# Graph attention on gathered neighbours: weighing a tile as a head and a tail, lists two tiles ahead, products from the last slot

## The chip, the cores and the metric

The kernel runs on one core of one Trainium2 chip. The metric is the device time of one execution in microseconds; it was taken three times for the kernel before. All engines have queues of their own, which run in order: TensorE (PE, its weight loads PEld), VectorE (DVE), ScalarE (ACT), GpSimd (POOL) and SyncE (SP).

## The reference

There are N = 4096 nodes with D = 128 numbers each, and a 0/1 matrix `adj` of which about 0.8% is set, so a row has some 32 neighbours. Layer 0 is graph attention with 8 heads, layer 1 takes quantiles over the neighbours' new values:

```python
Wh = einsum('nd,hde->hne', nodes, W)
f1, f2 = einsum('hnd,hd->hn', Wh, a1), einsum('hnd,hd->hn', Wh, a2)
e = leaky_relu(f1[:, :, None] + f2[:, None, :], 0.2)
att = softmax(where(adj > 0, e, -9e15), axis=-1)
h = elu(einsum('hnm,hmd->hnd', att, Wh))
cat = transpose(h, (1, 0, 2)).reshape(N, 8 * 128)
x1 = layernorm(nodes + elu(cat @ W1 + b1)) * gamma + beta
# layer 1: of each row's neighbours those at every ceil(n/2)-th place are removed;
# of the rest, for each of 128 columns, the values at the quantiles .25, .5, .75
out = s @ Wl.T + bl + x1      # s: half their mean, half the node's own x1
```

## The kernel before

The neighbours of a row are found first (`neighbours`, with `eights` and `best`: VectorE's MAX8 on keys that TensorE makes in PSUM, lines 561 to 614), as a record `rec` of up to 64 neighbour numbers, their count, the row's number and its f1. Rows are then ranked by their count (`rank_by_count`) and scattered to DRAM in that order, so that a tile of 128 rows has rows of nearly equal counts and few empty slots. This is done in three blocks of 4, 9 and 19 tiles (`BLOCKS`), and each tile has a fixed capacity (`CAPS`), rounded up to slots of 32, 16, 8 and 4 (`layers`): from 24 to 64 slots, 1180 in all.

Layer 0 of a tile has these steps:

- `read_lists` (line 767) loads the tile's records `R` (and `narrow` for layers under 32) on SP's queue, and VectorE turns them into index columns `idx` and the factors `f1x` (lines 776 to 809).
- `fetch_rows` (818) has POOL issue one indirect DMA (`gather`, line 178) for each slot: 128 rows of 136 numbers (x, and f2 of 8 heads) into one of 16 places of a buffer `G`. There are 6 such buffers.
- `attend` (843) weighs them. VectorE makes `z` = f1 + f2 and the leaky relu (858, 864), ScalarE its exp (865); TensorE sums it (`den`, 871), VectorE inverts (881, 882), TensorE spreads the inverse (`rz`, 886), VectorE multiplies (895) and spreads z to `wide` (902), one for each layer of slots. TensorE then makes one product for each slot (`y`, 913), which is the weighted sum of x. From there on the tile has 8 heads x 128 columns: in two halves of four heads, ScalarE copies y (927), TensorE multiplies with W (`hT`, 934), ScalarE and VectorE make the elu (943, 945, 946), and TensorE multiplies with W1 into `o` (948). `finish_x1` (969) adds and normalizes; POOL scatters x1 to DRAM (`x_d`, line 187).

`attend` is a generator that yields between steps. `step` (340) fetches one tile, then runs `attend` of the tile before from its beginning to its end. Within it, after the first yield, the lists of the tile after the fetched one are made (`soon`), and after each yield some pieces of another generator are run: the search for the next block's neighbours in blocks 0 and 1, and the lists of layer 1 (`lists_of_layer_1`, line 1009) in the last tiles of block 2. The pieces of a step (`quota`) are shared evenly over `STEPS` = 18 yields. DVE, PE, ACT and POOL run their instructions in the order in which they are written here (`manual_schedule`), so the order of these yields is the order of each queue.

PSUM is shared out so: `small` (den, then o) twice, `rz` once, `y` two banks, `hT` one, the keys two.

After layer 0 comes the sort: POOL gathers x1 rows of the neighbours (`vals`), and VectorE runs selection networks on them (`quantile_out`, line 1113). 

Of the kernel before, what the change touches and what calls it, by code (L numbers as in the profile page):

```python
# [9 lines left out]
F32 = mybir.dt.float32  # L10
BF16 = mybir.dt.bfloat16
I32 = mybir.dt.int32
AF = mybir.ActivationFunctionType
# [20 lines left out]
ROUNDS = L // 8  # L34
GROUP = 5
STEPS = 18
KEEP_MIN = 6.0
# [164 lines left out]
def kernel(  # L202
# [116 lines left out]

    weigh, store = [], []  # L320

# [17 lines left out]

    def step(fetch=None, soon=None, pieces=None, quota=0, first=False, among=()):  # L340
        if first:
            keep_x1(fetch)
        if fetch:
            weigh.append(fetch_rows(tc, attp, fetch, xt_d, list(among)))
        if not first:
            keep_x1(fetch)
        if len(weigh) > 1 or (weigh and not fetch):
            done = 0
            each = quota / STEPS
            for k, x1_t in enumerate(attend(tc, attp, pp, weigh.pop(0), consts)):  # L350
                if soon:
                    ready.append(prepare(*soon))
                    soon = None
                while done < min(quota, (k + 1) * each):
                    next(pieces, None)
                    done += 1
            store.append(x1_t)
            quota -= done
        if soon:
            ready.append(prepare(*soon))  # L360
        for _ in range(quota):
            next(pieces, None)
# [8 lines left out]
    with tc.manual_schedule(engines=ORDERED):  # L371
# [3 lines left out]
        for b, n in enumerate(BLOCKS):  # L375
# [12 lines left out]
            for i in range(n):  # L388
                among = []
                if last and 1 < i < n - 6:  # L390
                    among = [
                        (all_d, rec[:, t, 0:REC1], ranks[:, t : t + 1])
                        for t in range((i - 2) * NT // (n - 8), (i - 1) * NT // (n - 8))
                    ]
# [372 lines left out]
def read_lists(tc, ap, rec_d, i, cap, t, bad, narrow):  # L767
# [3 lines left out]

    R = ap.tile([P, REC], F32, name="R", bufs=4)
    rows = rec_d[ts(i, P), :]
# [4 lines left out]
    )  # L778
    mine = ap.tile([P, 1], I32, name="mine", bufs=7)
# [64 lines left out]
def attend(tc, ap, pp, fetched, consts):  # L844
# [7 lines left out]

    z = ap.tile([P, L, H], F32, name="z")
    layer = []
# [12 lines left out]

    den = pp.tile([P, 32 * H], F32, name="small", bufs=2)
    for i, (w, k, runs, f1v) in enumerate(parts):
# [9 lines left out]
    yield  # L879
    rden = ap.tile([4, 32 * H], F32, name="rden")  # L880
    nc.vector.tensor_scalar(rden, den[0:4, :], TINY, None, ALU.max)
# [17 lines left out]
    for i, (w, k, runs, f1v) in enumerate(parts):  # L899
# [9 lines left out]
        c = k * H  # L909
        for G, col, g0, m in runs:  # L910
            for g in range(g0, g0 + m):

                nc.tensor.matmul(  # L913
                    yf[:, ts(g, c)],
                    lhsT=G[:, col + g - g0, 0:D],
                    rhs=pf[:, ts(g, c)],
                    start=(i == 0 and g % (w // 2) == 0),
                    stop=(i == len(parts) - 1),
                    skip_group_check=True,
                )  # L920
                if g % 8 == 7:
                    yield

    o = pp.tile([P, 32 * H], F32, name="small", bufs=2)[:, 0:D]
    for h0 in range(0, H, 4):
        yT, hv, e = (ap.tile([P, 4, P], F32, name="half", bufs=4) for _ in range(3))
        nc.scalar.copy(  # L927
            yT.rearrange("p h (u g) -> p g u h", u=4),
            yf.rearrange("p (g u h) -> p g u h", u=4, h=H)[:, :, :, h0 : h0 + 4],
        )  # L930
        yield
        hT = pp.tile([P, 512], F32, name="hT")
        for h in range(4):
            nc.tensor.matmul(  # L934
                hT[:, ts(h, P)],
                lhsT=consts["W_sb"][:, h0 + h, :],
                rhs=yT[:, h, :],
                start=True,
                stop=True,
            )  # L940
        yield
        ef, hf = (v.rearrange("p h q -> p (h q)") for v in (e, hv))
        nc.scalar.activation(ef, hT, AF.Exp)  # L943
        yield
        nc.vector.tensor_scalar(ef, ef, 1.0, -1.0, ALU.min, ALU.add)  # L945
        nc.vector.tensor_tensor(hf, hT, ef, ALU.max)  # L946
        for h in range(4):
            nc.tensor.matmul(  # L948
                o,
                lhsT=hv[:, h, :],  # L950
                rhs=consts["W1_sb"][:, h0 + h, :],
                start=(h0 + h == 0),
                stop=(h0 + h == H - 1),
            )
        yield
    x1_t = ap.tile([P, D], F32, name="x1_t", bufs=4)
    yield from finish_x1(tc, ap, o, R[:, R_X : R_X + D], x1_t, consts)
# [429 lines left out]
```

## Time and profile before

| what | us |
|---|---|
| median of 3 runs (lowest, highest) | 3876.51 (3872.57, 3877.78) |
| the profiled execution: time, span | 4780.24, 4778.5 |
| z of tile 0 (end of setup) | 227 |
| z of tile 4 (block 1 begins) | 612 |
| z of tile 13 (block 2 begins) | 1444 |
| layer 0 ends, the sort begins | 2850 |
| busy: PE, DVE, ACT, POOL | 1355.3, 2676.4, 413.3, 2763.5 |

The profiled execution is one other execution, with the profiler on, and took 904 us more than the median. Times of single instructions and waits come from it. "A <- B" after an instruction's idle time says what ended the idle time: B, or "issue" where the profile shows no wait that ended just then, or "remote" where it can't tell the source. Ends of matmul records are modelled. A group of instructions is named by its line, engine, operation and tiles, with their shape.

### The profile page before, as it was taken

Reading aid. Unit: us, or ns where it says so; the run is one execution under the profiler, and the core shown is the slowest. Engines: PE = TensorE matmul, PEld = TensorE weight load, DVE = VectorE, ACT = ScalarE, POOL = GpSimd, SP = SyncE. Lnnn points to the kernel's source line nnn. Section 1 sums busy time; section 2 is a strip of 40 time slices with the busy share of each in tenths; the row PEclk is TensorE's granted clock in tenths of the full one; section 3 lists DMA queues with packets and bytes.
Section 4 is the critical chain, followed back from the end, with each engine's and each line's share of the span. In section 5 each row is a group of like instructions: output and inputs, shape, how many; then the busy total and the mean of one; then the engine's idle time right before and its main releaser. Section 6 shows DMA issues by size and latency. Waiting matters only on the chain. (4 is left out here: it accounts for less than half of the span.)

```text
span 4778.5 us, 22122 instructions
## 1 busy us (share of the span) xinstructions
PE 1355.3 (28%) x5429; PEld 1026.7 (21%) x5433; DVE 2676.4 (56%) x6455; ACT 413.3 (9%) x667; POOL 2763.5 (58%) x2388
## 2 busy tenths in 40 slices
PE   5373445556233443343424250000000000000010
PEld 2042333333232342232423240000000000000010
DVE  7463354554313111111134235687779999999868
ACT  2110111211000101100000010000000000000000
POOL 1534434334544454544444518888878888888883
PEclk9995555555555555555555555555555555555555
DMA  5321323321111111111111101111111111111110
GB/s 182 113 72 40 115 77 95 99 79 47 45 42 35 37 41 35 39 36 39 43 36 31 40 8 43 40 40 37 39 41 41 37 30 33 41 40 37 36 40 20
DMA packets 110282, 241.26 MB, mean 50 GB/s; under 512 B 46976, under 2 KB 63360, under 8 KB 101952
## 3 DMA queue, kind: packets, MB, share of 16 engines
q0 software_dynamic: 76160, 160.24, 12.5%
q10 hardware_dynamic: 9360, 67.18, 4.1%
q1 hardware_dynamic: 24624, 12.34, 1.1%
q8 instruction: 45, 0.74, 0.1%
q14 instruction: 93, 0.76, 0.1%
HBM read 228.44 MB, written 11.15 MB: 50 GB/s over the span
## 5 line engine op out<-in xcount | busy, mean ns | idle before, releaser
L178 POOL DMA_INDIRECT G<-xt_d,idx x1180 | 1130.7, 958 | 1285.2 <-issue 692.4
L178 POOL DMA_INDIRECT vals<-x_d,idx x1024 | 1423.4, 1390 | 314.5 <-issue 303.2
L1113 DVE TENSOR_TENSOR work<-work 128x256 f32<-128x256 f32 (+7 forms) x1168 | 922.0, 824 | 0.7
L913 PE MATMUL y<-wide,G 128*128 128x32 f32 (+3 forms) x2360 | 540.2, 410 | 234.2 <-DVE wide L902 137.9
L1113 DVE TENSOR_TENSOR work<-work,work 128x512 f32<-128x512 f32 (+4 forms) x820 | 584.7, 739 | 1.3
L1133 PE MATMUL st_ps<-dg,goal 128*128 128x128 f32 x286 | 71.1, 425 | 1794.4 <-DVE goal L1113 1430.9
L913 PEld LDWEIGHTS y<-wide,G 128*128 128x128 f32 x2360 | 516.8, 328 | 267.4 <-DVE wide L902 150.1
L945 DVE TENSOR_SCALAR half<-half 128x512 f32<-128x512 f32 x64 | 27.6, 432 | 915.3 <-ACT half L943 822.3
L1133 PEld LDWEIGHTS st_ps<-dg,goal 128*128 128x128 f32 x286 | 63.0, 321 | 1800.4 <-issue 1799.5
L563 DVE MAX8 first<-key 128x8 f32<-128x128 f32 x1024 | 228.0, 283 | 300.9 <-remote 132.6
L1113 DVE TENSOR_TENSOR work<-vals 128x768 f32<-128x768 f32 (+11 forms) x64 | 128.8, 2028 | 269.6 <-DMA vals<-x_d,idx 266.0
L948 PE MATMUL small<-W_sb,half 128*128 128x128 f32 x512 | 120.8, 410 | 484.7 <-DVE half L946 315.7
L596 PE MATMUL key<-sgn,markb 128*128 128x512 bf16 x255 | 151.0, 593 | 254.1 <-DVE first L563 105.0
L948 PEld LDWEIGHTS small<-W_sb,half 128*128 128x128 f32 x512 | 102.9, 298 | 503.9 <-DVE half L946 331.0
L934 PE MATMUL hT<-half,W_sb 128*128 128x128 f32 x512 | 116.1, 400 | 236.3 <-ACT half L927 143.7
L557 ACT ACTIVATE sgn<-adj_t 128x2048 bf16<-128x2048 int32 x64 | 122.1, 1907 | 555.0 <-PE key L596 387.1
L927 ACT COPY half<-y 128x512 f32<-128x512 f32 x64 | 65.5, 1023 | 1073.7 <-remote 536.5
L934 PEld LDWEIGHTS hT<-half,W_sb 128*128 128x128 f32 x512 | 103.9, 301 | 252.0 <-ACT half L927 153.6
L886 PE MATMUL rz<-rden,ownT 4*128 4x32 f32 (+3 forms) x436 | 112.3, 434 | 152.8 <-DVE rden L882 113.8
L599 PE MATMUL key<-parts,oneb 64*128 64x512 bf16 x256 | 149.1, 583 | 9.0 <-POOL parts L196 6.3
L1132 ACT ACTIVATE dg<-ident,wt 128x128 f32<-128x128 f32 x143 | 47.5, 393 | 1092.5 <-PE st_ps L1133 1008.4
L886 PEld LDWEIGHTS rz<-rden,ownT 4*128 4x128 f32 x436 | 98.4, 322 | 170.9 <-DVE rden L882 124.6
(178 smaller groups left out, 1773.0 us busy)
## 6 DMA issues: line engine op xcount, KB each, us to landing
adj_t<-in_adj_dram ACTq DMA_DIRECT2D x64, 1024.0 KB
G<-xt_d,idx POOLq DMA_INDIRECT x1180
vals<-x_d,idx POOLq DMA_INDIRECT x1024
R<-rec_d SPq DMA_DIRECT2D x128, 26.2 KB
xt_d<-rec SPq DMA_DIRECT2D x4, 544.0 KB
rec<-in_x_dram SPq DMA_DIRECT2D x4, 512.0 KB
W_sb<-in_L_gnn_W_dram SPq DMA_DIRECT2D x2, 512.0 KB
a_b<-in_L_gnn_a_dram SPq DMA_DIRECT2D x2, 512.0 KB
```

The lines of the kernel that those rows point to most:

```text
L178: nc.gpsimd.indirect_dma_start(out=dst, out_offset=None, in_=rows, in_offset=bass.IndirectOffsetOnAxis(ap=idx, axis=0),)
L557: nc.scalar.activation(sgn, adj_t, AF.Sign, accum_out=cnt[:, i : i + 1])
L563: nc.vector.max(first[:, ts(c0 // CW + c, 8)], key[:, ts(c, CW)])
L596: nc.tensor.matmul(key, lhsT=markb, rhs=sgn[:, ts(b, 512)], start=True, stop=False)
L599: nc.tensor.matmul(key, lhsT=oneb[0:64, :], rhs=parts[:, ts(r, 512)], start=False, stop=True)
L886: nc.tensor.matmul(rz[:, layer[i] * H : (layer[i] + w) * H], lhsT=ownT[w][:, r, :], rhs=rden.rearrange("p (g r h) -> p r g h", r=k // 4, h ...
L913: nc.tensor.matmul(yf[:, ts(g, c)], lhsT=G[:, col + g - g0, 0:D], rhs=pf[:, ts(g, c)], start=(i == 0 and g % (w // 2) == 0), stop=(i == le ...
L927: nc.scalar.copy(yT.rearrange("p h (u g) -> p g u h", u=4), yf.rearrange("p (g u h) -> p g u h", u=4, h=H)[:, :, :, h0 : h0 + 4],)
L934: nc.tensor.matmul(hT[:, ts(h, P)], lhsT=consts["W_sb"][:, h0 + h, :], rhs=yT[:, h, :], start=True, stop=True,)
L948: nc.tensor.matmul(o, lhsT=hv[:, h, :], rhs=consts["W1_sb"][:, h0 + h, :], start=(h0 + h == 0), stop=(h0 + h == H - 1),)
L1113: nc.vector.tensor_tensor(slots_of(dst, (j, c, s, m), size), slots_of(a, (i, c, s, m), size), slots_of(b, (i + d, c, s, m), size), op,)
L1133: nc.tensor.matmul(st_ps[:, u, :], lhsT=goal[:, (j * k + u) * D : (j * k + u + 1) * D], rhs=dg, start=(j == 0), stop=False,)
```

## The change

`attend` keeps its steps up to the products, then yields the word "summed"; what follows is the tail. In `step`, the tail of one tile and the head of the next are run in turns, one yield each, tail first, and the pieces after each turn. The tail works on all 8 heads at once: one copy of y of 128x1024, one exp, one elu, in two buffers `late`; hT has two banks of PSUM, and den and o share one PSUM tile `small`, made once. Lists are made two tiles ahead (`soon` names tile i + 2, and at the start of a block two tiles), for which `R`, `mine`, `idx` and `f1x` get more buffers. The products of a layer of slots run from the last slot to the first. `GROUP` (tiles whose records are completed at once) goes from 5 to 4, `STEPS` from 18 to 12. The lists of layer 1 start one tile later, and there is one more empty step at the end.

```diff
-GROUP = 5
-STEPS = 18
+GROUP = 4
+STEPS = 12
...
+    consts["small"] = pp.tile([P, 512], F32, name="small")
...
+            head = attend(tc, attp, pp, weigh.pop(0), consts)
+        active = [v for v in (tail.pop() if tail else None, head) if v]
+        k = 0
+        while active:
+            for v in list(active):
+                said = next(v)
+                if said == "summed":
+                    tail.append(v)
+                    active.remove(v)
+                elif said:
+                    store.append(said)
+                    active.remove(v)
+            ready.extend(prepare(*v) for v in soon)
+            soon = ()
+            k += 1
+            while done < min(quota, k * each):
+                next(pieces, None)
+                done += 1
...
-                soon = (b, i + 1, t0) if i + 1 < n else None
+                soon = [(b, j, t0) for j in ((1, 2) if i == 0 else (i + 2,)) if j < n]
...
-                if last and i == n - 6:
+                if last and i == n - 5:
...
-                    left = -(-LIST_PIECES // 5)
+                    left = -(-LIST_PIECES // 4)
...
-        for _ in range(4):
+        for _ in range(5):
             step()
...
-    R = ap.tile([P, REC], F32, name="R", bufs=4)
+    R = ap.tile([P, REC], F32, name="R", bufs=5)
...
-        idx = ap.tile([P, 32], I32, name="idx", bufs=6)
+        idx = ap.tile([P, 32], I32, name="idx", bufs=8)
...
-            f1x = ap.tile([P, H * 32], F32, name="f1x", bufs=7)
+            f1x = ap.tile([P, H * 32], F32, name="f1x", bufs=9)
...
-    den = pp.tile([P, 32 * H], F32, name="small", bufs=2)
+    small = consts["small"]
+    den = small[:, 0 : 32 * H]
...
-        for G, col, g0, m in runs:
-            for g in range(g0, g0 + m):
+        for G, col, g0, m in reversed(runs):
+
+            for g in reversed(range(g0, g0 + m)):
...
-                    start=(i == 0 and g % (w // 2) == 0),
+                    start=(i == 0 and g % (w // 2) == w // 2 - 1),
...
-                if g % 8 == 7:
+                if g % 8 == 0:
                     yield
...
+    yield "summed"
+
+    yT, hv = (ap.tile([P, H, P], F32, name="late", bufs=2) for _ in range(2))
+    nc.scalar.copy(
+        yT.rearrange("p h (u g) -> p g u h", u=4), yf.rearrange("p (g u h) -> p g u h", u=4, h=H)
+    )
+    yield
+    hT = pp.tile([P, 2, 512], F32, name="hT").rearrange("p a b -> p (a b)")
+    for h in range(H):
+        nc.tensor.matmul(
+            hT[:, ts(h, P)], lhsT=consts["W_sb"][:, h, :], rhs=yT[:, h, :], start=True, stop=True
+        )
+    yield
+    hf = hv.rearrange("p h q -> p (h q)")
+    nc.scalar.activation(hf, hT, AF.Exp)
+    yield
+    nc.vector.tensor_scalar(hf, hf, 1.0, -1.0, ALU.min, ALU.add)
+    nc.vector.tensor_tensor(hf, hT, hf, ALU.max)
+    o = small[:, 32 * H : 32 * H + D]
+    for h in range(H):
+        nc.tensor.matmul(
+            o, lhsT=hv[:, h, :], rhs=consts["W1_sb"][:, h, :], start=(h == 0), stop=(h == H - 1)
+        )
```

More of the change, by code (lines that the diff above doesn't have):

```diff
@@ L315 @@
     pp = tc.alloc_tile_pool(name="att_ps", bufs=1, space=PSUM)
-    weigh, store = [], []
+    weigh, store, tail = [], [], []
+    consts["small"] = pp.tile([P, 512], F32, name="small")
     narrow = {
@@ L338, in keep_x1, with step @@
             scatter(nc, x1_d, x1_t, r)
-    def step(fetch=None, soon=None, pieces=None, quota=0, first=False, among=()):
+    def step(fetch=None, soon=(), pieces=None, quota=0, first=False, among=()):
         if first:
@@ L346, in step @@
             keep_x1(fetch)
+        done = 0
+        each = quota / STEPS
+        head = None
         if len(weigh) > 1 or (weigh and not fetch):
[L348 to L360, printed above, removed]
+            head = attend(tc, attp, pp, weigh.pop(0), consts)
[16 more added lines that the diff above has]
+                done += 1
+        quota -= done
+        ready.extend(prepare(*v) for v in soon)
         for _ in range(quota):
@@ L389 @@
                 among = []
-                if last and 1 < i < n - 6:
+                if last and 2 < i < n - 5:
                     among = [
                         (all_d, rec[:, t, 0:REC1], ranks[:, t : t + 1])
-                        for t in range((i - 2) * NT // (n - 8), (i - 1) * NT // (n - 8))
+                        for t in range((i - 3) * NT // (n - 8), (i - 2) * NT // (n - 8))
                     ]
@@ L778, in read_lists @@
     )
-    mine = ap.tile([P, 1], I32, name="mine", bufs=7)
+    mine = ap.tile([P, 1], I32, name="mine", bufs=9)
     nc.vector.tensor_copy(mine, R.bitcast(I32)[:, R_OWN : R_OWN + 1])
@@ L850, in attend @@
     slots = sum(w for w, _, _, _ in parts)
-    z = ap.tile([P, L, H], F32, name="z")
+    z = ap.tile([P, L, H], F32, name="z", bufs=2)
     layer = []
@@ L879, in attend @@
     yield
-    rden = ap.tile([4, 32 * H], F32, name="rden")
+    rden = ap.tile([4, 32 * H], F32, name="rden", bufs=1)
     nc.vector.tensor_scalar(rden, den[0:4, :], TINY, None, ALU.max)
@@ L920, in attend @@
                 )
-                if g % 8 == 7:
+                if g % 8 == 0:
                     yield
[L924 to L929, printed above, removed]
-        )
[L931 to L955, printed above, removed]
@@ L956, in attend @@
-    x1_t = ap.tile([P, D], F32, name="x1_t", bufs=4)
+    yield "summed"
[8 more added lines that the diff above has]
+            hT[:, ts(h, P)], lhsT=consts["W_sb"][:, h, :], rhs=yT[:, h, :], start=True, stop=True
+        )
@@ L957, in attend @@
+    yield
[9 more added lines that the diff above has]
+        )
+    yield
+    x1_t = ap.tile([P, D], F32, name="x1_t", bufs=3)
     yield from finish_x1(tc, ap, o, R[:, R_X : R_X + D], x1_t, consts)
```

## The prediction

> **What bounds the kernel now.** I read the stretches first: each engine's busy time in setup, in the three blocks of tiles (the last block in two), and in the sort. Columns: stretch and length in us; busy us and instructions of PE, PEld, DVE, ACT, POOL; PE clock; DMA share; GB/s.
> ```profile
> 227.00:612.00 385.00, 197.20 (x717) 131.19 (x719) 182.75 (x686) 58.86 (x68) 161.31 (x168) 0.70 0.26 79
> 612.00:1444.00 832.00, 398.49 (x1464) 266.26 (x1465) 367.70 (x1356) 121.82 (x143) 346.23 (x360) 0.54 0.23 68
> 1444.00:2418.00 974.00, 365.15 (x1672) 327.83 (x1673) 185.68 (x450) 87.58 (x117) 495.96 (x513) 0.53 0.16 39
> 2418.00:2850.00 432.00, 179.06 (x810) 163.63 (x810) 166.61 (x645) 39.35 (x53) 154.95 (x163) 0.53 0.11 27
> ```
> No engine is full before 2850, so a chain of waits sets the pace there. The diff touches nothing after 2850 (sort, 1928 us). Block 0 is four tiles, block 1 nine (92 us each), the third stretch tiles 13 to 25 (75 us each), the fourth tiles 26 to 31 (72 us each).
>
> Second, the waits: who waited for whom, total us, times, longest.
> ```profile
> DVE half L945 <- ACT half L943: 822.3, 41, 77.5
> POOL G L178 <- issue: 692.4, 1124, 54.5
> POOL G L178 <- PE y L913: 540.2, 21, 56.6
> ```
> VectorE stands in the second half of a tile (L945), and behind it in its queue stand the next tile's z and the lists of the tile after. POOL stands for a G buffer that products must free (540 us), or for lists. Of the 692 us, about 1100 x 0.30 us = 330 is the fixed gap of each gather; the rest is waits for lists.
>
> Third, the timeline of tile 20, with gathers running, and of the last tile, with none.
> ```profile
> 1961.20 0.42 ACT L865 ACTIVATE z<-z 128x256 f32<-128x256 f32 x1 [1.27 <-DVE z L864]
> 1962.15 0.96 POOL L178 DMA_INDIRECT G<-xt_d,idx  x1 [17.96 <-issue]
> 1968.21 13.86 PE L913 MATMUL y<-wide,G 128*128 128x32 f32 x64 [1.84 <-DVE wide L902]
> 2006.17 1.01 ACT L927 COPY half<-y 128x512 f32<-128x512 f32 x1 [44.56 <-remote]
> 2018.83 0.60 ACT L943 ACTIVATE half<-hT 128x512 f32<-128x512 f32 x1 [11.65 <-remote]
> ...
> 2817.72 13.86 PE L913 MATMUL y<-wide,G 128*128 128x32 f32 x64 [1.84 <-DVE wide L902]
> 2831.62 1.02 ACT L927 COPY half<-y 128x512 f32<-128x512 f32 x1 [20.30 <-PE y L913]
> 2844.02 0.29 DVE L974 TENSOR_TENSOR v<-small,vecs 128x128 f32<-128x128 f32 x1 [1.25 <-PE small L948]
> ```
> Both records say 13.86 us for 64 product records. In the last tile the copy follows at once; in tile 20 it starts 24 us later, and tile 20's gathers for the next tiles fill that time. So TensorE finishes late while gathers run: 38 us for 13.9, a factor of 2.75.
>
> [...] That would make the lag a matter of profiling. The trace does not prove it, but the time speaks for it: the profiled execution took 4780.24 us, the median of three unprofiled runs is 3876.51, 904 us less. [...]
>
> **So two sums.** With TensorE at its unhindered pace, a 32-slot tile takes what the last one took: z at 2809.3, copy at 2831.6 (22), end at 2847.7 (16), 38 us. POOL needs 0.95+0.30 = 1.25 us an instruction: 513 x 1.25 = 641 us for tiles 13 to 25, 49 a tile, more than 38. There POOL is the pace, and 974 shrinks by 333. Block 1: POOL 360 x 1.25 / 9 = 50 a tile; VectorE 41. A tile costs between 50 and 38 + 33 (the searching, 294 us / 9, with nothing hidden), I take 56 plus 60 in all for the block's records: 832 shrinks by some 270. Block 0 likewise by 80, the fourth stretch by 80. Together 760 of the 904; the sort may give the rest. This fits, so I forecast on the unhindered sum, against 3876.51; the sum as profiled is given as a rival.
>
> **Part by part.**
> 1. *Tail beside the next head.* Nothing is removed from the tail: two copies of 1.02 become one of 2.04, two exps of 0.60 one of 1.19, L945 2 x 0.43, L946 2 x 0.69 become about 0.86 and 1.23, 8 + 8 weight products stay 32 records x 0.213 = 6.8 us. Estimated from z to the last product: 22 us alone, plus hT's 3.4 us ahead of den on TensorE, plus 0.86 + 1.23 on VectorE and o's 3.4 ahead of the products, less overlap: 28. On ScalarE the copy's 2.04 stands ahead of the head's exp; it is within the 3.4. The pace of the chain is 28 instead of 38. The scatter of x1 (1.0 us on POOL) is issued one step later, and nothing waits for it before the sort: 0.
>  Block 1: from 56 to 51, since POOL's 50 is next: 9 x 5 = 45. Block 0: 4 x 6 = 24 by the same share. Tiles 13 to 25: 0, POOL is hidden by nothing. Tiles 26 to 31: list pieces are 98 us of VectorE, some 16 a tile; 38 to 45 + part of 16 is above POOL's 34 (163 x 1.25 / 6), so 4 tiles x 7 = 28. The last tile: head 28 beside tail 30, then its own tail 16, but it starts 16 earlier: 9 less. Gain: 106.
> 2. *Lists two tiles ahead.* Takes away POOL's waits for lists (17.96 in the line above). With POOL as pace they are already gone: 0 beyond part 1. The DMAs are as many (R four issues, 1.7 us on SP; narrow four, 1.3 us) and stand on SP's queue with nothing else; R is kept for the tail and has a fifth buffer, so no load waits for it. VectorE's 2.2 us of transposes stay in front of rden. But the ring idx has 8 buffers and tiles 14 to 16 take 3 each, so list 16 waits for 16 gathers of tile 14, 16 x 1.25 = 20 us, VectorE behind it with rden. Once; between 0 and 20, I take 10.
> 3. *Products from last to first.* 0 in TensorE's time. G's first buffer comes free after 32 products instead of 16, 16 x 0.427 = 6.8 us later. Hidden as long as head + gather < two tiles: 28 + 50 < 100. The waits themselves: the records run at 0.213 with and without one, so 0.
> 4. *GROUP 4.* One more group in blocks 1 and 2, 24 small VectorE instructions of about 0.2 each: 2 x 4.8, hidden if POOL is the pace. Between 0 and 10, I take 5. *STEPS 12* only shares the pieces over fewer turns; what is left after the last turn runs beside the next copy: 0, at worst two pieces of 2 us a step, 13 x 4 = 52.
> 5. *PSUM:* hT takes two banks, den and o share one tile. den of the next head must wait until v (L974) has read o; that is a full head earlier: 0.
>
> Sum: 106 - 10 - 5 = 91 less; 3876.5 - 91 = 3785. I say 3783, as the ends are rounded.
>
> **Rivals.**
> A. *TensorE lags beside gathers without a profiler too.* For it: the trace shows it in every tile. Against: the sort cannot give 904 us by itself without VectorE's 1649 us of it shrinking by more than half. As profiled, a tile costs gather time plus the TensorE work that it could not do meanwhile: tiles 13 to 25: 24 us of work, 49 + 24 - 49/2.75 = 55 against 75, 13 x 20 = 260; block 1: 42 of work, 74 against 92, 160; elsewhere 100. 520 of 4780, 11%. Half true, 5 to 7%: 3876 - 250 = 3630.
> B. *The gathers set the pace everywhere.* Then parts 1 and 2 only shorten what was hidden; 3876 + 0 to 15, about 3880. For it: POOL's 50 a tile in block 1 is close to my 56. Against: 60 us of VectorE per tile in block 0 can't be hidden in 52.
> C. *Slower: G comes free too late.* The place is POOL's wait for y, in the 18 tiles with over 32 slots, which need three buffers or more of six. A gather starts when the first buffer of two tiles back is free, lasts 50, and the head needs it. With a head stretched by pieces, as in blocks 0 and 1, the pace is half of gather + 2 + head; it passes 56 when the head passes 60 us. The trace has 43 to 85 us from z to the copy in block 1 (though with TensorE lagging). Price 18 x 6.8 / 2 = 61 at least where two tiles share a delay, 122 where each pays it, with some of part 1's gain left: 3876 + 40 = about 3915.
>
> **How the numbers follow.** Forecast (3700 to 3860): 0.48. A (3560 to 3700): 0.25. B: 0.12, mostly within 0.2%. C: 0.15. About 0.2%, 8 us, is what a measurement of this kernel can tell from no change. Faster: 0.48 + 0.25 and a little of B, 0.74; same 0.09; slower 0.17. Range 3610 to 3895: it takes in most of A and B, and the near end of C.
>
> **What would show it.** In the profile after, beside gathers: L945 waits far less for L943; POOL goes from one tile's gathers to the next's with under 5 us between, where it now waits 18 to 20; from z to z some 55 to 60 us in tiles 13 to 25; z to the last product longer than before, the copy of y in the next turn. Its own time near 4300 would not contradict a small gain unprofiled. C would show as waits of POOL for y no less than 540 us and longer each. I am wrong if the unprofiled time falls by more than 250 us (A), or if tiles 13 to 25 were never paced by POOL, or if VectorE stands for idx for more than one tile.

## The result, and the profile after

The kernel after the change took **3857.37 us** (median of seven runs, 3844.21 to 3882.75), the kernel before 3877.78 us beside it (3872.57 to 3880.68): a ratio of **0.9954, 95% interval 0.9937 to 0.9972**, some 18 us or 0.46% faster. The forecast was 3783 us, so the direction was right and the size was not: 94 us were promised, 20 came. The profiled execution of after took 3857.37 us too, with a span of 3855.5 us; it shows none of the lateness of TensorE that the prediction saw in the profile of before. The runs below come from several chips, and on three of them every execution was late beside the gathers, as the profile shown of before was (before takes 4729 to 4785 us there), on the others none was (before takes 3877 to 3880 us); "late" marks the first kind.

For this reason the profile of before is no good partner of the profile after. The experiment b_rev is: it is the kernel before with nothing but y's products reversed, it takes before's time (ratio 1.0010), and its execution was not late. The stretches below run from the exp of z (ScalarE, line 876, in b_rev line 865) of one tile to that of another: tiles 0 to 4 (block 0), 4 to 13 (block 1), 13 to 25, 25 to 31, and from there to the sort. Columns as in the prediction: stretch, length, busy us and instructions of PE, PEld, DVE, ACT, POOL, the PE clock, the DMA share, GB/s. First b_rev:

```profile
161.00:445.00 284.00, 192.98 (x719) 128.74 (x719) 183.15 (x687) 58.69 (x68) 193.00 (x200) 0.61 0.38 114
445.00:1019.00 574.00, 382.59 (x1466) 258.54 (x1467) 369.79 (x1358) 122.10 (x144) 342.57 (x352) 0.57 0.33 98
1019.00:1602.00 583.00, 328.47 (x1533) 295.50 (x1533) 172.72 (x412) 80.45 (x107) 432.59 (x446) 0.55 0.24 56
1602.00:1911.00 309.00, 181.68 (x848) 166.04 (x848) 174.38 (x656) 40.61 (x54) 231.36 (x238) 0.55 0.23 55
```

Then after:

```profile
164.00:446.00 282.00, 182.11 (x699) 119.10 (x700) 184.42 (x707) 53.52 (x56) 191.57 (x196) 0.67 0.37 113
446.00:982.00 536.00, 354.10 (x1458) 244.94 (x1457) 367.16 (x1358) 119.28 (x125) 340.45 (x344) 0.60 0.35 104
982.00:1577.00 595.00, 307.01 (x1547) 281.63 (x1545) 163.69 (x380) 77.25 (x86) 458.34 (x449) 0.58 0.21 54
1577.00:1888.00 311.00, 165.23 (x848) 152.06 (x848) 167.41 (x632) 38.61 (x43) 236.31 (x240) 0.57 0.23 59
```

Read the lengths first. Block 1 went from 574 to 536 us: 38 us gained. Block 0 went from 284 to 282, with its start 3 us later: nothing. Tiles 13 to 25 went from 583 to 595: 12 us lost. Tiles 25 to 31: 2 lost, and 1 more on the way to the sort. Together 38 - 1 - 12 - 2 - 1 = 22 us, within rounding the difference of the two spans (3878.3 and 3855.5). The sort takes 1926 us in b_rev, 1925 in after and 1928 in the profile of before. Then read POOL in the third line: in tiles 13 to 25 it has 449 instructions of mean 1.02 us, and with 0.30 us between each two they fill 458 + 135 = 593 of 595 us. Nothing else comes near. In b_rev the same sum is 433 + 134 = 567 of 583 us (446 instructions): POOL was nearly full there before, and its instructions take 26 us longer in after. This is the stretch whose bound the change could not move.

The waits of after, for the whole execution (engine, line, tile, whom it waited for: us in all, times, longest):

```profile
DVE z L869 <- DMA G<-xt_d,idx: 468.5, 40, 25.1
POOL G L178 <- issue: 339.9, 1114, 0.6
DVE bad L787 <- DMA R<-rec_d: 105.8, 6, 57.3
POOL G L178 <- PE y L926: 99.8, 10, 32.4
DVE late L952 <- ACT late L950: 16.7, 1, 16.7
```

VectorE no longer stands in the tail: its wait for the exp (822 us in the profile of before, 413.5 in b_rev) is 16.7 us, once. It now stands at the start of a head, for gathers. POOL's waits without a releaser are 0.30 us each, the longest 0.6: it goes from gather to gather and never waits for lists. Its waits for y are 99.8 us.

The timeline of tile 20, the one that the prediction showed (start, us, engine, line, what it does, idle time before it):

```profile
1316.74 0.38 DVE L869 TENSOR_TENSOR z<-G,f1x 128x128 f32<-128x128 f32 x1 [23.19 <-DMA G<-xt_d,idx]
1317.61 0.42 ACT L876 ACTIVATE z<-z 128x256 f32<-128x256 f32 x1 [20.85 <-DVE z L875]
1326.99 13.70 PE L926 MATMUL y<-wide,G 128*128 128x32 f32 x64
1340.78 1.87 ACT L939 COPY late<-y 128x1024 f32<-128x1024 f32 x1 [10.95 <-PE y L926]
```

The 64 products again take 13.7 us by their records, and here the copy of y follows their end at once (1340.69, 1340.78), where it came 24 us late before. The head, from z to the last product, takes 24 us, and each z waits for its tile's gathers (23.19 us here).

### The profile page after: what moved, and what is told of

It reads as the page before. It is cut to its first block, busy times and chain, and to the rows that moved or that the text cites. A ratio compares the mean times of both kernels' runs of the same rounds, so it can differ in the third digit from the quotient of the medians.

```text
span 3855.5 us, 21960 instructions
## 1 busy us (share of the span) xinstructions
PE 1253.7 (33%) x5433; PEld 961.2 (25%) x5433; DVE 2671.4 (69%) x6439; ACT 403.4 (10%) x603; POOL 2807.9 (73%) x2388
## 5 line engine op out<-in xcount | busy, mean ns | idle before, releaser
L178 POOL DMA_INDIRECT G<-xt_d,idx x1180 | 1173.6, 995 | 483.4 <-issue 339.9
L926 PE MATMUL y<-wide,G 128*128 128x32 f32 (+3 forms) x2360 | 480.1, 382 | 21.9 <-DVE wide L914 21.9
L926 PEld LDWEIGHTS y<-wide,G 128*128 128x128 f32 x2360 | 460.0, 297 | 45.8 <-DVE wide L914 24.2
L869 DVE TENSOR_TENSOR z<-G,f1x 128x128 f32<-128x128 f32 (+2 forms) x92 | 29.9, 335 | 471.6 <-DMA G<-xt_d,idx 468.5
L607 PE MATMUL key<-sgn,markb 128*128 128x512 bf16 x256 | 142.0, 555 | 160.9 <-DVE first L574 107.5
L883 PE MATMUL small<-z,own 128*4 128x32 f32 (+3 forms) x436 | 50.4, 284 | 368.1 <-ACT z L876 368.1
L956 PE MATMUL small<-W_sb,late 128*128 128x128 f32 x512 | 118.9, 426 | 33.6 <-DVE late L953 33.6
L187 POOL DMA_INDIRECT out_dram<-o,own_i x32 | 67.9, 2123 | 79.9 <-ACT o L1163 56.2
L883 PEld LDWEIGHTS small<-z,own 128*4 128x4 f32 x436 | 27.1, 102 | 385.8 <-ACT z L876 373.3
L956 PEld LDWEIGHTS small<-W_sb,late 128*128 128x128 f32 x512 | 110.2, 327 | 44.9 <-DVE late L953 43.9
```

The costliest lines, as they stand in the source:

```text
L178: nc.gpsimd.indirect_dma_start(out=dst, out_offset=None, in_=rows, in_offset=bass.IndirectOffsetOnAxis(ap=idx, axis=0),)
L187: return nc.gpsimd.indirect_dma_start(out=rows, out_offset=bass.IndirectOffsetOnAxis(ap=idx, axis=0), in_=src, in_offset=None,)
L607: nc.tensor.matmul(key, lhsT=markb, rhs=sgn[:, ts(b, 512)], start=True, stop=False)
L883: nc.tensor.matmul(den[0:4, :].rearrange("p (g r h) -> p r g h", r=k // 4, h=H)[:, r], lhsT=own[w][:, ts(r, 4)], rhs=z[:, layer[i] : layer ...
L926: nc.tensor.matmul(yf[:, ts(g, c)], lhsT=G[:, col + g - g0, 0:D], rhs=pf[:, ts(g, c)], start=(i == 0 and g % (w // 2) == w // 2 - 1), stop ...
L956: nc.tensor.matmul(o, lhsT=hv[:, h, :], rhs=consts["W1_sb"][:, h, :], start=(h == 0), stop=(h == H - 1))
```

## The experiments

All are compared with the kernel before on the same chip.

**The parts of the change, one by one.** b_rev is before with the products reversed; b_lists adds the lists two ahead and GROUP 4, with the buffers of after (more for the lists, one `rden` in place of two, three `x1_t` in place of four); a_fwd is after with the products in the old order; a_one is after with lists one ahead.

```diff
# b_rev, in the kernel before (start flags and yields are turned round with it, as in after)
-        for G, col, g0, m in runs:
-            for g in range(g0, g0 + m):
+        for G, col, g0, m in reversed(runs):
+            for g in reversed(range(g0, g0 + m)):
# b_lists, besides (and R, mine, idx, f1x, rden, x1_t with the buffers of after)
-GROUP = 5
+GROUP = 4
-                soon = (b, i + 1, t0) if i + 1 < n else None
+                soon = [(b, j, t0) for j in ((1, 2) if i == 0 else (i + 2,)) if j < n]
# a_fwd: b_rev's edit taken back in after; a_one, in after
-                soon = [(b, j, t0) for j in ((1, 2) if i == 0 else (i + 2,)) if j < n]
+                soon = [(b, i + 1, t0)] if i + 1 < n else []
```

> The kernel before with one edit: the products of a layer run from the last slot to the first. Theory (the slow TensorE beside gathers was a matter of the profiled execution[...]): unprofiled as before, 3868 to 3886 us, and the profiled execution now within 20 us of that instead of 904 above; in it the sort takes 1925 us, tiles 13 to 31 are paced by POOL as in the changed kernel (z to z within 2 us of it), and the 20 us that the change won lie ahead of tile 13. Rival 1 (the waits slow TensorE without a profiler too): 3850 to 3865, that is, this edit alone is the gain. Rival 2 (G comes free later, a cost): 3890 to 3920.

> The kernel before with the products reversed and the lists made two tiles ahead (R, mine, idx, f1x as in the changed kernel; GROUP 4, one rden and three x1_t to make room), without head and tail. Theory: POOL waits for lists only ahead of tile 13, where VectorE is late: 3860 to 3880, 0 to 15 below b_rev. Rival (the lists are the whole gain): as the changed kernel, 3857, or less.

> The changed kernel with its products run forward again. Theory: unprofiled 3847 to 3867, as the changed one; the profiled execution slow again, 4250 or more, with copies of y late beside gathers. Rival 1: 3870 to 3885 unprofiled. Rival 2 (late G costs the changed kernel in block 1, where POOL waited 84 us for y): 3815 to 3840.

> The changed kernel with lists one tile ahead again, head and tail and the order kept. Theory (most of the gain is head and tail in blocks 0 and 1): 3855 to 3870; the wait of 17 us for the ring idx goes, POOL waits for lists in blocks 0 and 1 come back. Rival (lists are the gain): 3872 to 3885. The other rival (lists two ahead cost more than they bring, as VectorE stands for R in the block's first step): 3830 to 3850.

Measured: b_rev 1.0010 (1.0001 to 1.0018), b_lists 1.0054 (1.0041 to 1.0066), a_fwd 0.9952 (0.9936 to 0.9968), a_one 0.9962 (0.9949 to 0.9976). So the reversal is worth nothing either way: put into before it costs some 3 us, taken out of after it changes nothing. Lists two ahead are worth some 4 us in after at most (3863.6 us with one ahead, beside 3859.6 for after with forward products; their intervals overlap). In before, lists, GROUP 4 and the buffers together cost 16 us, 12 of them ahead of block 1: the z of tile 4 comes at 457 us in b_lists, 445 in b_rev. What is gained comes with head and tail and what belongs to them (their buffers, PSUM and STEPS were not tried apart from them): a_one, which has them without the lists two ahead, comes to the z of tile 13 at 980 us, after at 982, b_rev at 1019.

**Is the late execution an accident?**

> The kernel before, unchanged, profiled once more. Its first profiled execution took 4780 us against 3878 unprofiled, while the four other builds profiled so far stand within 3 us of their own times. Theory: TensorE's lag beside the gathers (tiles 13 to 25 in 974 us, against 584 in the same program with y in the other direction) belongs to this build when it is profiled, so it comes back: a span of 4600 to 4800 us. Rival: it was an accident of one execution: a span of 3875 to 3885 us. The unprofiled time is about 3878 us under both.

Measured: 4722.07 us, and the eleven runs of before beside it took 4740.55 us (4724.22 to 4759.32). The stretches of before_again, for the same tiles (0 to 4, 4 to 13, 13 to 25, 25 to 31):

```profile
228.00:601.00 373.00, 193.74 (x719) 128.45 (x719) 182.69 (x685) 58.58 (x68) 162.67 (x168) 0.60 0.27 81
601.00:1420.00 819.00, 396.52 (x1465) 265.56 (x1465) 367.75 (x1357) 121.84 (x143) 346.64 (x360) 0.54 0.24 69
1420.00:2292.00 872.00, 338.70 (x1533) 302.94 (x1533) 172.55 (x418) 80.91 (x108) 456.80 (x472) 0.53 0.17 40
2292.00:2756.00 464.00, 184.50 (x848) 169.01 (x848) 170.14 (x656) 41.00 (x55) 192.63 (x203) 0.54 0.13 32
```

The busy times are near those of b_rev (but for POOL, which does part of its work further ahead), the lengths are 89, 245, 289 and 155 us more. It came back, as the theory said, but not for the theory's reason: the eleven runs beside it are as late, and so are the three variants of after that ran on the same chip (below). So it belongs neither to the build nor to one execution. It goes with the chip, or with something else that all runs of one occasion share: no chip was used on two. Every run has a span and a clock reading, on both kinds of chip, so no run is known to have been free of the recording of traces.

**The ring of idx, the held gathers, the first G buffer.** Three edits of after, each for one loss that its profile suggested: nine idx buffers (a_idx), min and -1 by a two-input instruction in place of the one-input one (a_stt), y's products from the first G buffer on (a_runs).

```diff
# a_idx
-        idx = ap.tile([P, 32], I32, name="idx", bufs=8)
+        idx = ap.tile([P, 32], I32, name="idx", bufs=9)
# a_stt (ones: a column of ones in SBUF, broadcast)
-    nc.vector.tensor_scalar(hf, hf, 1.0, -1.0, ALU.min, ALU.add)
+    nc.vector.scalar_tensor_tensor(hv, hv, 1.0, ones, ALU.min, ALU.subtract)
# a_runs
-        for G, col, g0, m in reversed(runs):
+        for G, col, g0, m in runs:
```

> The changed kernel with nine idx buffers instead of eight. Theory: the 17.3 us for which VectorE stands for a gather that still reads idx (at 987 us) cost the 13 us lost between tiles 13 and 17, so the time falls by 8 to 17 us, to about 3843 to 3850 us, and tile 17's z comes near 1165 instead of 1176 us. Rival: the gathers set the pace there anyway, and the wait is hidden: within 3 us of 3857, tile 17's z still at 1174 to 1177 us.

> The changed kernel with exp's min and -1 done by a two-input instruction (a row of ones as second input) instead of the one-input TENSOR_SCALAR 128x1024 that took 0.62 us; VectorE works about 0.6 us longer in each of 32 tiles. Theory: it is the fast one-input form behind the reciprocal that holds a gather for 1.5 us; with the slower form the gathers of tiles 18 to 31 are not held, their mean falls from 1001 towards 967 ns, and the time falls by 8 to 15 us, to 3842 to 3849 us. Rival 1: any long run of VectorE instructions holds a gather: then 0.6 us more of it in each tile makes the kernel slower by 5 to 20 us. Rival 2: the stretched gathers cost nothing, as POOL isn't the pace: within 3 us of 3857.

> The changed kernel with y's products taken G buffer by G buffer from the first (inside a buffer still from last to first), so that the first buffer comes free some 7 us earlier. Theory: POOL's 100 us of waits for y (10 times, the longest 32.4) in tiles 8 to 12 are hidden behind VectorE's search: within 5 us of 3857. Rival (the third of the prediction): the late G buffer sets the pace of block 1: 10 waits fall by 7 us each, and half to all of that shows, 3790 to 3825 us.

They ran on a late chip: 0.9433 (0.9400 to 0.9466), 0.9427 (0.9395 to 0.9459), 0.9414 (0.9384 to 0.9445). None of the expected microseconds can be read from that, because all were meant for an execution that isn't late. They ran again with after beside them, and again the chip was a late one; a_best has all three edits.

> The changed kernel itself, beside the kernel before. Where before takes about 3877 us: 3857 us again (ratio 0.993 to 0.997). Where before takes about 4740 us, as in the last comparison, with TensorE late beside the gathers: 4440 to 4490 us (ratio 0.937 to 0.947), as its three variants took, since none of their edits touches what is slow there.

> The changed kernel with nine idx buffers once more, to be set beside the changed kernel itself. Theory: where before takes about 3877 us, 8 to 17 us less than the changed kernel, with tile 17's z near 1165 us. Rival: within 3 us, the wait is hidden behind the gathers. Where before takes about 4740 us: within 10 us of the changed kernel under both, as the gathers aren't the pace there.

> The changed kernel with the two-input form in place of the one-input TENSOR_SCALAR 128x1024 once more. Theory: where before takes about 3877 us, the gathers beside the reciprocal go from 2.5 us back to about 1 us, and the time is 8 to 15 us under the changed kernel's. Rival 1: any long run of VectorE instructions holds a gather: 5 to 20 us more. Rival 2: within 3 us. Where before takes about 4740 us: the gathers' durations tell the first two apart in the profile, and the time is within 10 us.

> Nine idx buffers, the two-input form, and y's products buffer by buffer from the first, in one kernel. If the stall for idx and the held gathers each cost what they seem to, 16 to 35 us less than the changed kernel (3822 to 3841 us) where before takes about 3877 us; if the gathers' pace hides both, within 5 us of it. Where before takes about 4740 us: within 20 us of the changed kernel.

Measured: after_again **0.9348** (0.9325 to 0.9370), a_idx_2 0.9338 (0.9310 to 0.9365), a_stt_2 0.9391 (0.9363 to 0.9419), a_best 0.9363 (0.9339 to 0.9387). The time of after_again is where it was expected, its ratio is 0.002 below, since before took 4785 us. So where executions are late, the same change is worth 315 us (4785 to 4470), some fifteen times the 20 us that it is worth elsewhere. The stretches of after_again, to be set beside those of before_again on another late chip:

```profile
251.00:604.00 353.00, 184.40 (x694) 121.30 (x696) 183.10 (x701) 52.75 (x55) 157.38 (x162) 0.66 0.28 83
604.00:1357.00 753.00, 361.10 (x1464) 243.08 (x1464) 368.77 (x1362) 120.41 (x127) 357.92 (x369) 0.57 0.27 76
1357.00:2050.00 693.00, 298.95 (x1535) 278.72 (x1535) 162.97 (x382) 77.35 (x83) 424.76 (x424) 0.57 0.19 43
2050.00:2488.00 438.00, 168.19 (x850) 155.88 (x849) 164.09 (x625) 39.20 (x43) 224.05 (x234) 0.56 0.17 41
```

Of the 265 us between these two profiled executions, 179 are in tiles 13 to 25, where the other kind of chip loses 12. That fits a chain of late work, which overlapping two tiles shortens, against gathers that fill POOL, which it does not; no run takes the two apart. The two-input form is no gain: 20 us slower than after on the same chip, where at most 10 were expected (on the first late chip it took 8 us less than a_idx). Neither it nor a_runs ran where executions are not late. The profile of a_stt_2 tells more than its time. A gather beside the reciprocal, in the timeline of a_stt_2:

```profile
1849.48 1.74 DVE L895 RECIPROCAL rden<-rden 4x256 f32<-4x256 f32 x1
1850.75 2.37 POOL L178 DMA_INDIRECT G<-xt_d,idx  x1 [0.30 <-issue]
1851.15 1.15 DVE L954 SCALAR_TENSOR_TENSOR late<-late,ones 128x1024 f32<-128x1024 f32 x1
1852.33 1.23 DVE L955 TENSOR_TENSOR late<-hT,late 128x1024 f32<-128x1024 f32 x1
```

It is held as it was in the timeline of after:

```profile
1319.81 1.74 DVE L894 RECIPROCAL rden<-rden 4x256 f32<-4x256 f32 x1
1320.44 2.47 POOL L178 DMA_INDIRECT G<-xt_d,idx  x1 [0.30 <-issue]
1321.48 0.62 DVE L952 TENSOR_SCALAR late<-late 128x1024 f32<-128x1024 f32 x1
1322.13 1.23 DVE L953 TENSOR_TENSOR late<-hT,late 128x1024 f32<-128x1024 f32 x1
```

In both, the gather ends 0.8 us after the second of the three VectorE instructions does: 1322.10 and 1322.91 here, 1852.30 and 1853.12 there. A gather elsewhere takes 0.95. So the theory of a_stt, that a gather is free once the one-input form, 0.62 us long, is gone, has fallen, and its first rival, that longer work of VectorE holds it longer, is what the profile shows: of two gathers that began 1.27 us into a reciprocal, the one in after (at 1581.0 us) took 1.83 us, the one above in a_stt_2 2.37, and the instruction behind the reciprocal takes 0.62 and 1.15. The third instruction, which reads PSUM, holds nothing (0.94 to 0.96 us for the 26 gathers that began beside it in after).

**Moving the instruction away, and the pace of the gathers.** In a_order the tail's min, -1 and max come one turn earlier, ahead of the reciprocal; a_oi has nine idx buffers besides; a_direct has plain loads of consecutive rows in place of all 1180 gathers (its expectation says 1124). These ran on a chip that isn't late, with after beside them.

```diff
# a_order, and in a_oi besides a_idx's edit
     nc.scalar.activation(hf, hT, AF.Exp)
-    yield
     nc.vector.tensor_scalar(hf, hf, 1.0, -1.0, ALU.min, ALU.add)
# a_direct
-            gather(nc, G[:, col, :], xt_d, idx[:, g : g + 1])
+            nc.sync.dma_start(G[:, col, :], xt_d[ts(g % NT, P), :])
```

> The changed kernel, to compare the next two with. About 3857 us where before takes about 3877 us, about 4460 to 4480 us where before takes about 4740 to 4790 us.

> The changed kernel with the tail's min, -1 and max one turn earlier: on VectorE they stand ahead of the reciprocal, not right behind it. Theory: a gather is held when a wide instruction waits right behind another one, so the gathers of 1.8 to 3.0 us beside the reciprocal are gone in the profile (at most 1.6 us each there), and where before takes about 3877 us the time is 6 to 14 us under the changed kernel's. Rival: any row of three busy VectorE instructions holds a gather, in whatever order: the held gathers move to the new place and cost the same, within 3 us. Second rival: o's products now stand ahead of rz's on TensorE and the head is 3.4 us later in each tile: 5 to 20 us slower where before takes about 4740 us.

> The last one with nine idx buffers as well. Theory: both losses of tiles 13 to 31 are separate, so where before takes about 3877 us it is 8 to 17 us under the one before it, 3828 to 3842 us. Rival: the gathers' pace hides the wait for idx: within 3 us of it. Where before takes about 4740 us: within 10 us of it.

> The changed kernel with each of the 1124 gathers of a tile's slots replaced by a plain load of 128 consecutive rows of the same table, issued by SP: the same bytes in the same rows of 544 B, no indirect address, nothing on POOL in a tile but the scatters. (What it leaves out is the choice of the rows.) Theory 1, the indirect gathers themselves set the pace of tiles 13 to 31, at 1.25 us each, and hold the other engines up where the engines are late: the sort starts 250 to 450 us earlier where before takes about 3877 us (3400 to 3600 us in all), and where before takes about 4740 us the lateness is gone and the time is the same 3400 to 3600 us. Theory 2, the traffic of the rows does it: the start of the sort moves by less than 100 us on either kind of chip.

Measured: after_third 0.9963 (0.9950 to 0.9977), a_order **1.0031** (1.0019 to 1.0044), a_oi 1.0032 (1.0021 to 1.0044), a_direct 3559.32 us in one run. In a_order the held gathers are gone, as its theory said: all 37 that began beside a reciprocal took 0.94 to 0.96 us. The same place in its timeline, tile 20:

```profile
1308.53 1.29 POOL L178 DMA_INDIRECT G<-xt_d,idx  x1 [0.30 <-issue]
1309.05 0.65 DVE L951 TENSOR_SCALAR late<-late 128x1024 f32<-128x1024 f32 x1
1315.12 0.94 POOL L178 DMA_INDIRECT G<-xt_d,idx  x1 [0.30 <-issue]
1315.35 1.74 DVE L894 RECIPROCAL rden<-rden 4x256 f32<-4x256 f32 x1
```

Between the z of tiles 17 and 31 all four executions issue 543 instructions to POOL's DMA queue. Their mean is 968 ns in b_rev, 1001 in after, 1003 in after_third and 967 in a_order, and the stretch takes 696, 711, 713 and 693 us. 543 x 33 ns = 18 us, of which the ten gathers held beside a reciprocal make 15: they are the whole of what after loses there, and a_order has it back. Yet a_order is 27 us slower than after beside it. Now o's products stand ahead of the next head: 'rden' waits 3.88 us for them (line 893, tile 20), and comes 8 us after z where it came after 2; in the whole execution it waits 110 us for them, 31 times. In tiles 17 to 31 the gathers hide that. In blocks 0 and 1 nothing does: from z of tile 0 to z of tile 13 it takes 865 us, after_third 825. The second rival was right on the loss, though it looked for it on the other kind of chip.

a_oi equals a_order (3891.25 and 3891.65 us), as its rival said: the ninth idx buffer gains nothing, so VectorE's 17 us for idx are hidden behind the gathers.

a_direct falls within the range of its first theory: 305 us less than after_third, with the sort beginning 301 us earlier. Its stretches:

```profile
168.00:442.00 274.00, 181.46 (x697) 117.97 (x698) 182.12 (x705) 53.48 (x55) 13.51 (x12) 0.68 0.38 112
442.00:964.00 522.00, 358.17 (x1462) 247.50 (x1462) 364.00 (x1362) 120.00 (x127) 31.83 (x28) 0.60 0.38 108
964.00:1342.00 378.00, 288.00 (x1536) 267.59 (x1536) 160.60 (x373) 77.40 (x84) 48.35 (x44) 0.65 0.37 86
1342.00:1592.00 250.00, 173.11 (x850) 162.17 (x850) 162.47 (x634) 39.41 (x44) 7.21 (x6) 0.58 0.26 62
```

Without indirect gathers, tiles 13 to 31 take 628 us instead of 906, and blocks 0 and 1 only 22 us less than in after. So POOL's gathers set the pace of tiles 13 to 31 and little of the pace before. (a_direct changes two things at once, who issues the loads and which rows they read; that POOL's instructions fill tiles 13 to 25 in after speaks for the first.) What a_direct would do where executions are late was not seen.

**Two last ones**, both on a late chip: a_order's edit in the last block alone (a_mix), and after with STEPS back at 18 (a_steps).

```diff
# a_mix (early is true in the steps of the last block alone)
-    yield
+    if not early:
+        yield
     nc.vector.tensor_scalar(hf, hf, 1.0, -1.0, ALU.min, ALU.add)
# a_steps
-STEPS = 12
+STEPS = 18
```

> The changed kernel, with the tail's min, -1 and max ahead of the reciprocal only in the steps of the last block, where POOL's gathers set the pace; blocks 0 and 1 stay as they are. Theory: the 18 us that tiles 18 to 31 gained come without the 36 us that blocks 0 and 1 lost, so the time is 12 to 20 us under the changed kernel's: ratio to before 0.990 to 0.993 where before takes about 3877 us. Rival: the later head costs in the last block too, ratio 0.996 or more. Where before takes about 4740 to 4790 us, TensorE's order decides instead: 0 to 30 us over the changed kernel's.

> The changed kernel with STEPS back at 18. A step of head and tail has some 12 turns, so a third of a step's pieces would be left for its end. If the pieces at the end run beside gathers and products anyway, within 5 us of the changed kernel (ratio 0.994 to 0.998 where before takes about 3877 us); if they stand bare on VectorE, 10 to 50 us slower (ratio 0.998 to 1.01).

Measured: a_mix 0.9542 (0.9518 to 0.9566), a_steps 0.9378 (0.9350 to 0.9406). a_mix is worse than after (0.9348 on another late chip, and 72 us slower than a_steps beside it) by more than the 0 to 30 us that were expected there; where executions aren't late, where 12 to 20 us were expected from it, it was not tried. So a version that beats after was not shown. a_steps is within the spread of after, a_idx, a_stt and a_runs on late chips (0.9338 to 0.9433): no cost or gain of STEPS can be told from that.

## Why the prediction was right or wrong

**The base was good, its reason was not.** The prediction took the profile of before for a disturbed one and estimated an undisturbed one: block 1 shorter by 270 us, tiles 13 to 25 by 333, block 0 by 80, the last stretch by 80. Against b_rev, cut at the same tiles, they are 258, 344, 101 and 128 us. It missed the 66 us before the first z, and looked for the rest in the sort, which gives 2. But it put the lateness down to the profiler; that was the author's estimate, from one profiled execution that took 904 us more than the median of three others, and no trace showed it. That the base held owes nothing to this reason. What the runs show is that all runs of a chip agree: eleven runs of before took 4740 us, eleven 4785 and eleven 4729 on three chips, beside 29 that took 3877 and 48 that took 3880 on two others. Executions with a trace stand on both sides, so the division into profiled and unprofiled runs, made ahead of the prediction and in it, is not what separates them. That the recording of traces plays a part on the late chips is neither shown nor excluded (last section).

**Part 1, head and tail, is the term that failed: 106 us were counted, 22 measured.** It took the chain of a tile for the pace in block 0 and in the last tiles, where shortening it gained nothing, and it put the change's price on POOL's queue at nothing.
- Block 1: 45 foreseen, 38 measured. From 574 us to 536, where 564 (nine times 56, and 60 for the records) to 519 was foreseen: level and step nearly right.
- Block 0: 24 "by the same share", measured -1. There is no share to carry over. Nor do lists two ahead hide a gain: a_one, which has head and tail without them, takes 284 us from the z of tile 0 to that of tile 4, as b_rev does. What sets the pace there stays open; without gathers (a_direct) it is still 274 us.
- Tiles 26 to 31 and the last one: 28 + 9 foreseen, -3 measured. This is the worst line of the sum. It held POOL's need to be 34 us a tile, from 163 instructions in that stretch, divided by six. But the stretch begins with the z of tile 26, whose own gathers lie ahead of it, and in a late execution POOL is further ahead of the other engines, and had done more of these tiles' gathers before (from tile 25's z to tile 31's it has 203 instructions in before_again, 238 in b_rev). The slots are fixed: 36, 40, 40, 40, 44 and 32, together 232, or 48 us a tile at 1.25 us each; b_rev's records from tile 25's z to tile 31's have 238 POOL instructions, which with 0.30 us between them fill 303 of 309 us. So POOL is the pace there, not the tile's own chain, and there is next to nothing to gain.
- Tiles 13 to 25: 0 foreseen, "POOL is hidden by nothing". The bound was right, but the change made it slower: 12 us, not priced at all. Two elementwise instructions of half the width became one of full width, right behind the reciprocal, and one gather in each of these twelve tiles takes 1.88 to 2.98 us instead of 0.95, 18 us in all. The traces show which instructions go with a longer gather: the one-input TENSOR_SCALAR behind the reciprocal (17 gathers of after, 1.83 to 2.98 us), the two-input instruction in its place in a_stt_2 (2.37 us above), and the two-input tensor_tensor that makes `wide`, in before as in after (up to 1.83 and 1.94 us for gathers that began beside it). The reciprocal of b_rev (43 gathers) and the instruction that reads PSUM (26 gathers of after) go with none: 0.94 to 0.96 us. One thing more is told below. By what means a gather is held was not shown. The prediction priced the wider instructions on VectorE alone, not on the queue beside it.

**Part 2, lists:** 0, right. The stall for idx was seen as priced, 17.3 us once, for a foreseen 0 to 20, but where it was taken away (a_oi against a_order) nothing was gained, since POOL had gathers in hand: the deduction of 10 was wrong. **Part 3, reversal:** 0, right (b_rev, a_fwd). **Part 4:** GROUP 4 at 5; with lists and buffers it costs 16 in before, and it was not tried alone. STEPS was tried on a late chip only. **Part 5:** 0; no line of the waits speaks against it.

With its measured terms the sum is 38 - 1 - 12 - 3 = 22 in place of 91.

**The rivals.** B, gathers set the pace everywhere, is what holds in tiles 13 to 31, not before them (a_direct). The prediction's figure against it, 60 us of VectorE per tile in block 0, does not come from its own line, which has 182.75 us for four tiles, 46 each. A (late beside gathers) is right on late chips in kind, not in size, and whether it would be so without a trace, as it says, can't be told: 315 us against the 520 that it gave for a wholly late execution, 66 against 160 in block 1, 179 against 260 in tiles 13 to 25. C did not come: POOL's waits for y are 99.8 us in after, 66.5 in b_rev, and taking the buffers in the old order gains nothing (a_fwd).

**What was to show it:** POOL passes from tile to tile in 0.3 us (under 5 foreseen), z to z is 50 us in tiles 13 to 25 (55 to 60 foreseen), the copy of y comes in the next turn.

## What to carry to other kernels

Before an overlap is priced, count the bounding queue's work of each stretch from the program (slots times the measured time of one), not from the records that fall into the stretch: an engine that runs ahead leaves its work in the stretch before. Where GpSimd's gathers set the pace, look there for the price of a wide VectorE instruction, and of where it stands: here a TENSOR_SCALAR of 128x1024 right behind the reciprocal held a gather by 1.5 us a tile, one turn earlier the mean gather was as short as before (967 and 968 ns), though the turn cost more elsewhere. And where a profiled execution and the other runs differ by a quarter, take both once more on one chip before explaining it.

## What the runs showed of the hardware that was not expected

**A gather was held from before the wide instruction started.** First a gather of after, then one of b_rev:

```profile
1473.47 1.74 DVE L894 RECIPROCAL rden<-rden 4x256 f32<-4x256 f32 x1
1473.59 2.98 POOL L178 DMA_INDIRECT G<-xt_d,idx  x1 [0.30 <-issue]
...
1308.51 1.74 DVE L882 RECIPROCAL rden<-rden 4x256 f32<-4x256 f32 x1
1309.20 0.94 POOL L178 DMA_INDIRECT G<-xt_d,idx  x1 [0.30 <-issue]
```

The first began 0.12 us into the reciprocal and took 2.98 us, though it needed 0.95 and the wide instruction started only at 1475.14 us. The reciprocal by itself holds none: the 43 gathers that began beside it in b_rev took 0.94 to 0.96 us. In after it depends on what stands behind the reciprocal. Where it is the wide TENSOR_SCALAR, all 17 gathers that began 0.12 us or more into the reciprocal took 1.83 to 2.98 us; where it is another instruction (a MAX8 of the search, a narrow one of the lists), all 17 took 0.94 to 0.95. So the gather is held already while the wide instruction is still next in line behind the reciprocal, though it began 1.55 us ahead of that instruction (1473.59 and 1475.14 us). How, the traces don't show.

**Executions of this program come in two kinds, 22% apart, with the sort alike in both.** Eleven late executions were traced, on three chips and in the profile of before, and nine others. In the late ones 702 to 788 of the engines' semaphore updates have no record, in the others none to 4; of the updates that DMAs make, the late traces hold 19,796 to 20,745, the others 42,330 to 42,484, of the same 2,721 DMA issues. In phases with gathers the engines stand longer in the late ones: in a_idx the first z comes at 250 us, in after at 164, though the gathers of that tile run from 114 to 154 in both, and TensorE is busy for 10.0 us of those 40 in a_idx, for 25.5 in after. What links the missing records to the lateness, if anything does, no run here tells; instructions' own durations (1.74 us for the reciprocal of tile 20 in before and in after) and the gathers' 0.95 us are the same in both.
